# A PixArt block on one core: VectorE makes the low part of the contexts' query tokens, POOL adds the epsilon, and one small transfer goes ahead of another

## The chip, the core and the metric

The kernel runs on one core of a Trainium2 chip. The metric is the time of one execution on the device, in microseconds (us). The five engines have their own instruction queues and run side by side: TensorE (PE in the profile, with its weight loads as PEld), VectorE (DVE), ScalarE (ACT), GpSimd (POOL), and SyncE (SP), which here does nothing but issue transfers.

## What is computed

A transformer block over 16 samples of 256 tokens with 256 features, with a context of 256 tokens for each sample. Cut to what matters:

```
x_norm = modulate(_ln(x), shift_a, scale_a)
q, k, v = split(x_norm @ W_qkv + b_qkv)          # 16 heads of 16 features
x = x + gate_a * (softmax(q k^T * scale) v @ W_proj + b_proj)
q_c = _ln(x) @ W_qc + b_qc
k_c, v_c = split(_ln(context) @ W_kvc + b_kvc)
x = x + softmax(q_c k_c^T * scale) v_c @ W_cproj + b_cproj
h = gelu(modulate(_ln(x), shift_m, scale_m) @ W_mlp1 + b_mlp1)
x = x + gate_m * (h @ W_mlp2 + b_mlp2)
```

`_ln` is (x - mean) / sqrt(var + 1e-6). The change concerns `_ln(x)` ahead of `W_qc`: the tokens from which a context attention makes its queries.

## The kernel before

**Units and beats.** There are 32 attentions: for each sample one over its own tokens (kind "s") and one over its context (kind "c"). Each is a unit. They stand in the order s0 to s4, then s5, c0, s6, c1, ... s15, c10, and then c11 to c15 alone (lines 783 to 798). The main loop (lines 1241 to 1253) goes through the units, and through eight beats 0 to 7 in each; `beat(n, k)` (line 1073) writes out by hand what is issued in beat k of unit n. All engines keep the order in which the code is written. Behind the units stands the MLP, 16 samples in four chunks each.

**What a beat holds.** `visit` (line 1049) issues four matmuls of scores of the *next* unit into the PSUM tile `s` (`s_tile`, line 690) and four matmuls of transposed scores of the current unit into `st` (`t_part`). One VectorE reduction then takes the maxima of `s` (the tile `mx`), and one ScalarE instruction makes exponentials of `st` (the tile `pt`). There is one tile `s`, so the matmuls into it in a beat wait until the reduction of the beat before has read it; and `st` likewise waits for the exponentials. The even beats also hold 16 matmuls of probabilities by values (`av_part`, tile `o`) and the odd beats 24 matmuls of projections for units that are to come or that are done (`lanes`).

**Preparing a unit.** The unit n+3 is called q3, n+4 is q4; `lx` is q3 if it is a context unit, `lc` is q4 if it is one, `ls` is q4 if it is an "s" unit. For a context unit two layernorms are made: one of the context (`lc.ln[0]`, names with `_c`) and one of the tokens after the first attention (`lc.ln[1]`, names with `_q`). A layernorm (line 309) has three steps: `stats` (VectorE's bn_stats, tile `st_q`), `rstd` (VectorE's bn_aggr, tile `mv_q`, and then `pow`, tile `rs_q`: add epsilon, raise to -0.5) and `apply` (POOL, two instructions, tile `xn_q`). Adding epsilon is POOL's for samples 0 to 7 and VectorE's for samples 8 to 15 (the list `eased`, line 307); raising to the power is POOL's always.

**High and low part.** The normalized tokens are transposed by TensorE into PSUM (tile `psT_q`, in beat 4) and split in two numbers of lower precision: the high part `xTh_q` (ScalarE, `high`, line 385) and what is left, the low part `xTl_q`. For the context's query tokens ScalarE copies PSUM to the SBUF tile `y_q` (`full`, line 405), since POOL doesn't read PSUM here, and POOL subtracts (`rest_pool`, line 413). The function `low` (line 395) does the subtraction on VectorE, straight from PSUM; in `parts` (line 422) it is the third entry, and before the change it is used for the "s" units alone. Both parts are used in beat 1 of the next unit (tile `ps_qc`).

**Two rows on SP's queue.** In beat 0 the negated maxima of the second half (`m_row`, tile `m_1`) are sent into a row of the queries' tile, where beat 4 first uses them, and the softmax sums of the unit before are gathered (`pull_sums`, tile `S`). Their reciprocal is VectorE's in beat 2 (or 3, if q4 is an "s" unit); VectorE waits there if they have not landed.

**Where two context units follow each other.** For n = 23 to 28 the unit n+3 is a context unit, and for n = 23 to 27 so is the unit n+4. These six units then hold the work of `lx`, and all but the last also that of `lc`; before n = 23, units with the one and with the other alternate. `late` (line 1085) is set where `lc` is the first or the last sample.

Of the kernel before, what the change touches and what calls it, by code (L numbers as in the profile page):

```python
# [21 lines left out]
def pixart_block(  # L22
# [281 lines left out]
    class Box:  # L304
        pass

    eased = [f"{c}{b}" for c in "cq" for b in range(8, B)]

    def layernorm(src, name):

        o = Box()

        def stats():
            o.st = work.tile([P, NT, 6], F32, tag="bnst", bufs=4, name=f"st_{name}")
            for t in range(NT):
                DVE.bn_stats(o.st[:, t], src()[:, t])

        def rstd(power=True):
            o.mv = work.tile([P, NT, 2], F32, tag="bnmv", bufs=4, name=f"mv_{name}")
            for t in range(NT):  # L320
                DVE.bn_aggr(o.mv[:, t], o.st[:, t])
            o.rs = work.tile([P, NT], F32, tag="rstd", bufs=4, name=f"rs_{name}")
            if power:
                o.pow()

        def pow():
            if name in eased:
                DVE.scalar_tensor_tensor(o.rs, o.mv[:, :, 1], EPS, o.mv[:, :, 1], ALU.add, ALU.max)
            else:
                POOL.tensor_scalar(o.rs, o.mv[:, :, 1], EPS, None, ALU.add)  # L330
            POOL.tensor_tensor(o.rs, o.rs, mhalf, ALU.pow)

        def apply(eng=E_['LN'].get(name[0])):
            o.xn = work.tile([P, NT, H], F32, tag="xn", name=f"xn_{name}", bufs=3)
            if eng == "act":
                nb = work.tile([P, NT], F32, tag="rstd", name=f"nb_{name}", bufs=4)
                DVE.scalar_tensor_tensor(nb, o.mv[:, :, 0], -1.0, o.rs, ALU.mult, ALU.mult)
            for t in range(NT):
                if eng == "act":
                    ACT.activation(o.xn[:, t], src()[:, t], AF.Identity, bias=nb[:, t:t + 1],  # L340
                                   scale=o.rs[:, t:t + 1])
                else:
                    (DVE if eng == "dve" else POOL).tensor_scalar(
                        o.xn[:, t], src()[:, t], o.mv[:, t, 0:1], o.rs[:, t:t + 1],
                        ALU.subtract, ALU.mult)

        def apply_half(t):
            if t == 0:
                o.xn = work.tile([P, NT, H], F32, tag="xn", name=f"xn_{name}", bufs=3)
                POOL.tensor_scalar(o.xn[:, t], src()[:, t], o.mv[:, t, 0:1], o.rs[:, t:t + 1],  # L350
                                   ALU.subtract, ALU.mult)
            else:
                ACT.activation(o.xn[:, t], src()[:, t], AF.Identity, bias=o.nb[:, t:t + 1],
                               scale=o.rs[:, t:t + 1])

        def apply_bias():
            o.nb = work.tile([P, NT], F32, tag="rstd", name=f"nb_{name}", bufs=4)
            DVE.scalar_tensor_tensor(o.nb, o.mv[:, :, 0], -1.0, o.rs, ALU.mult, ALU.mult)

        o.apply_half, o.apply_bias = apply_half, apply_bias  # L360

        def stat(t):
            if t == 0:
                o.st = work.tile([P, NT, 6], F32, tag="bnst", bufs=4, name=f"st_{name}")
            DVE.bn_stats(o.st[:, t], src()[:, t])

        o.steps, o.pow, o.stat = [stats, rstd, apply], pow, stat
        return o

# [351 lines left out]
    def m_turn(u, hf, pst=None):  # L721

        if pst is None:
            pst = ps_gen(f"psm_{u.n}_{hf}", SHORT)
        PE.transpose(pst[:16, :P], u.mx[:, hf].rearrange("p r a t -> p (r a t)"), ident)
        return pst
# [25 lines left out]
    def exps():  # L752

        for f in later:
            f()
        later.clear()
# [316 lines left out]
    def beat(n, k):  # L1073
# [29 lines left out]
        if k == 0:  # L1103
            exps()
            if prev:
                av_part(prev, 3)
            if q3 and q3.ready:
                q3.T[0].place()
                pst = m_turn(cur, 1, q3.T[0].ps[:, N:])
                q3.T[0].turn((0,))  # L1110
            else:
                pst = m_turn(cur, 1)
            m_row(cur, 1, pst)
            if q2:
                q2.K.low()
            if prev:
                p1.pull_sums(1)
            if q2:
                q2.K.send_low()
            if p2:  # L1120
                p2.norm()
                p2.high()
                p2.low()
        elif k == 1:
            exps()
            run(lanes(q2 and q2.Q, q2 and n and q2.V))
            if prev:
                p1.pull_values(1)
            if lc:
                lc.ln[0].steps[0]()  # L1130
            if lx:
                if lx.b in (0, B - 1):
                    lx.ln[1].steps[0]()
                lx.ln[1].steps[1]()
                if lx.b == B - 1:
                    lx.ln[1].apply_half(0)
                else:
                    lx.ln[1].steps[2]()
        elif k == 2:
            exps()  # L1140
            if cur:
                av_part(cur, 0)
            if q3:
                q3.T[0].turn((1,) if q3.ready else (0, 1))
            if ls:
                ls.ln[0].steps[0]()
            elif prev:
                p1.recip()
                p1.spread()
            if not (q3 and q3.kind == "c"):  # L1150
                spare(n)
        elif k == 3:
            if q3:
                q3.T[0].high()
            exps()
            if q3 and q3.kind == "c":
                q3.T[0].full()
            if alone and p2:
                p2.proj(0)
                p2.proj(1)  # L1160
            elif n:
                run(lanes(p2, q2 and q2.Q))
            else:
                run(lanes(q2.V, q2.Q))
            if q3 and q3.kind == "s":
                q3.T[0].low()
            if prev and ls:
                p1.recip()
                p1.spread()
            if lx and lx.b == B - 1:  # L1170
                lx.ln[1].apply_bias()
        elif k == 4:
            if lx and lx.b == B - 1:
                lx.ln[1].apply_half(1)
            exps()
            if alone:
                p2.end()
            if cur:
                av_part(cur, 1)
            if lx:  # L1180
                lx.T[1].turn()
            if nxt:
                m_part(nxt, 0, st[:, 0] if lx else None)
            if q2:
                q2.Q.low()
                q2.Q.send_low()
            if q3 and q3.kind == "c":
                q3.T[0].rest_pool()
                spare(n, not lc)
            if ls:  # L1190
                ls.ln[0].steps[1]()
                ls.ln[0].steps[2]()
                ls.ready = True
        elif k == 5:
            exps()
            run(kp or lanes(q3 and q3.K, (None if alone else p2) if n else q2.V))
            if cur:
                o_out(cur, 0)
            if lc:
                lc.ln[0].steps[1]()  # L1200
                lc.ln[0].steps[2]()
                lc.ready = True
            v = unit(n + 5)
            if v and v.kind == "c":
                load(v)
            if prev:
                p1.back()
        elif k == 6:
            exps()
            if lx:  # L1210
                lx.T[1].high()
            if cur:
                cur.post.begin()
                av_part(cur, 2)
                cur.post.pull(0)
            if q3 and p2:
                q3.vk = lanes(q3.V, q3.K)
                run(q3.vk, 1)
            if p3:
                p3.store()  # L1220
            if lx:
                lx.T[1].full()
                lx.T[1].rest_pool()
                if lc:
                    p1.gate()
        elif k == 7:
            exps()
            run(q3.vk if q3 and p2 else lanes(q3 and q3.V, q3 and q3.K))
            if late:
                p2.add()  # L1230
                p2.added = True
            elif lc:
                lc.ln[1].steps[0]()
            v = unit(n + 5)
            if v and v.kind == "s":
                load(v)
            if n == nu - 1:
                p2.add()
                p2.store()
# [102 lines left out]
```

## Time and profile before

| | us |
|---|---|
| runs shown (three) | 730.75, 727.42, 733.64; median 730.75 |
| profiled execution, its own time | 729.14 |
| its span, first to last instruction | 727.3 |
| busy: PE, PEld, DVE, ACT, POOL | 712.7, 593.4, 566.5, 556.9, 538.9 |

The own time is 1.84 us more than the span, which lies around it. Rows of the timeline read: start in us, duration in us, engine, line, operation, tile written <- tiles read, shape, count, and in brackets the idle time of the engine before it with what ended it. Nearly all instructions carry line 51, that of the helper that records them, so the tiles' names tell them apart. Windows of time give the busy us of each engine in a stretch, with the number of its instructions.

### The profile page before, as it was taken

What the parts mean: (1) busy time and instruction counts of PE and PEld (TensorE: products, weight loads), DVE (VectorE), ACT (ScalarE), POOL (GpSimd) and SP (SyncE); (2) the same over time, 40 slices, a digit from 0 to 9 for tenths busy, and PEclk for the clock granted to TensorE, in tenths of its full rate; (3) what the DMA queues carried; (4) which work ended last, traced back from release to release, by engine and by line L of the source; (5) the groups of instructions that cost most, each with busy time, mean ns of one, the idle gap of its engine ahead of it and who ended that gap; (6) DMA issues with size and microseconds to landing.
All of it is one profiled execution on the core that took longest, in us unless ns stands there. A gap on an engine that the chain in (4) does not pass through costs nothing.

```text
span 727.3 us, 22494 instructions
## 1 busy us (share of the span) xinstructions
PE 712.7 (98%) x9007; PEld 593.4 (82%) x9007; DVE 566.5 (78%) x892; ACT 556.9 (77%) x971; POOL 538.9 (74%) x517
## 2 busy tenths in 40 slices
PE   9999999999999999999999999999999999999996
PEld 8777777877877778777777777777679999999996
DVE  4878888888887888888889888878675777777743
ACT  5677888888888888888888878888767677666661
POOL 8555788887866868787786797988767988666561
PEclk9999999999999999999999999999999999999999
DMA  7465455544545455454555645455332223213122
GB/s 253 151 223 172 151 173 169 186 170 164 166 149 185 155 188 194 157 164 164 192 170 181 205 152 178 149 183 184 97 88 94 89 59 88 72 61 89 52 51 73
DMA packets 81531, 106.14 MB, mean 146 GB/s; under 512 B 16594, under 2 KB 44532, under 8 KB 81428
## 3 DMA queue, kind: packets, MB, share of 16 engines
q1 hardware_dynamic: 80420, 104.12, 43.9%
q8 instruction: 71, 1.16, 0.7%
q10 hardware_dynamic: 1008, 0.59, 0.3%
q14 instruction: 32, 0.26, 0.1%
HBM read 35.89 MB, written 8.98 MB: 62 GB/s over the span
## 4 chain that ended last, share of the span: by engine, by line
PE 89%; DVE 5%; ACT 2%; DMA 1%; issue 1%; SPq 0%; ACTq 0%
PE s L51 18%; PE o L51 15%; PE st L51 14%; PE ph L51 12%; DVE mx L51 4%; PE ps_v_c L51 3%; PE ps_k L51 3%; PE ps_q L51 3%; PE ps_kc L51 3%; PE ps_P_s L51 3%; PE ps_v_s L51 3%; PE ps_qc L51 2%; PE ps_P_c L51 2%; PE psT_s L51 2%; PE psT_c L51 1%
## 5 line engine op out<-in xcount | busy, mean ns | idle before, releaser
L51 DVE TENSOR_REDUCE mx<-s 128x4 f32<-128x1024 f32 x252 | 308.0, 1222 | 81.2 <-PE s L51 79.5
L51 ACT ACTIVATE pt<-st 128x1024 f32<-128x1024 f32 x256 | 264.6, 1033 | 54.3 <-PE st L51 52.9
L51 PE MATMUL o<-pt,v 128*32 128x256 f32 x2048 | 137.0, 385 | 0.0
L51 PE MATMUL s<-big 63*128 63x256 f32 x1008 | 117.2, 306 | 6.2 <-DVE mx L51 5.0
L51 PE MATMUL st<-big 64*128 64x256 f32 (+1 forms) x1040 | 109.6, 285 | 0.7 <-ACT pt L51 0.7
L51 PE MATMUL ph<-xTh_m,wself 128*128 128x256 f32 x512 | 99.5, 280 | 0.0
L51 PEld LDWEIGHTS s<-big 63*128 63x128 f32 x1008 | 77.4, 185 | 25.5 <-DVE mx L51 11.2
L51 POOL TENSOR_TENSOR hl<-hf,hh 128x512 fp32r<-128x512 f32 x60 | 81.4, 1375 | 19.4 <-ACT hh L51 19.4
L51 PEld LDWEIGHTS o<-pt,v 128*32 128x32 f32 x2048 | 53.4, 109 | 39.4 <-ACT oT L51 0.8
L51 PEld LDWEIGHTS st<-big 64*128 64x128 f32 (+1 forms) x1040 | 81.2, 186 | 4.4 <-ACT pt L51 2.1
L51 PEld LDWEIGHTS ph<-xTh_m,wself 128*128 128x128 f32 x512 | 81.9, 188 | 1.2 <-issue 0.4
L51 PE MATMUL ph<-xTl_m,wself 128*128 128x256 f32 x256 | 70.9, 277 | 0.0
L51 ACT ACTIVATE hh<-ph,bT 128x256 fp32r<-128x256 f32 x112 | 47.4, 479 | 19.0 <-PE st L51 7.4
L51 ACT ACTIVATE hf<-ph,bT 128x256 f32<-128x256 f32 x112 | 47.2, 475 | 19.1 <-PE ph L51 19.0
L51 PEld LDWEIGHTS ph<-xTl_m,wself 128*128 128x128 f32 x256 | 48.2, 188 | 0.0
L51 PE MATMUL s<-big,hh 128*128 128x256 f32 x256 | 45.2, 277 | 0.0
L51 DVE TENSOR_SCALAR xn_m<-x,mv_m,rs_m 128x256 f32<-128x256 f32 x28 | 33.5, 1237 | 14.8 <-POOL rs_m L51 14.8
L51 POOL TENSOR_SCALAR xn_c<-c,mv_c,rs_c 128x256 f32<-128x256 f32 x32 | 39.0, 1228 | 1.7
L51 PE MATMUL st<-big,hh 128*128 128x256 f32 x224 | 39.5, 276 | 0.0
L51 POOL TENSOR_SCALAR xn_q<-x,mv_q,rs_q 128x256 f32<-128x256 f32 x31 | 37.8, 1228 | 1.7
L51 PEld LDWEIGHTS s<-big,hh 128*128 128x128 f32 x256 | 38.7, 188 | 0.0
L51 ACT COPY oT<-o 128x512 f32<-128x512 f32 x64 | 37.5, 587 | 1.4 <-PE o L51 1.4
(231 smaller groups left out, 2127.0 us busy)
## 6 DMA issues: line engine op xcount, KB each, us to landing
big<-h_kc SPq DMA_DIRECT2D x32, 256.0 KB
big<-h_qc SPq DMA_DIRECT2D x32, 256.0 KB
big<-h_k SPq DMA_DIRECT2D x31, 256.0 KB
big<-h_q SPq DMA_DIRECT2D x30, 256.0 KB
big<-l_k SPq DMA_DIRECT2D x16, 256.0 KB
g<-gd SPq DMA_DIRECT2D x16, 256.0 KB
U_s<-oT SPq DMA_DIRECT2D x32, 128.0 KB
c<-in_ctx_dram SPq DMA_DIRECT2D x16, 256.0 KB
```

The source lines that it names most:

```text
L51: i = f(*a, **k)
```

## The change

Four things are edited. Sixteen copies `y_q` by ScalarE and sixteen subtractions by POOL go away, and VectorE's `low` makes `xTl_q` from PSUM, in beat 7 instead of beat 6. The sixteen epsilon additions of `eased` go from VectorE to POOL. In beat 0 the gathering of the sums is issued on SP's queue ahead of the maxima's row. And where a unit has both `lx` and `lc`, the statistics `st_q` of `lc` are taken in beat 6 instead of beat 7.

```
-    eased = [f"{c}{b}" for c in "cq" for b in range(8, B)]
...
         def pow():
-            if name in eased:
-                DVE.scalar_tensor_tensor(o.rs, o.mv[:, :, 1], EPS, o.mv[:, :, 1], ALU.add, ALU.max)
-            else:
-                POOL.tensor_scalar(o.rs, o.mv[:, :, 1], EPS, None, ALU.add)
+            POOL.tensor_scalar(o.rs, o.mv[:, :, 1], EPS, None, ALU.add)
             POOL.tensor_tensor(o.rs, o.rs, mhalf, ALU.pow)
...
                 pst = m_turn(cur, 1)
+            if prev:
+                p1.pull_sums(1)
             m_row(cur, 1, pst)
             if q2:
                 q2.K.low()
-            if prev:
-                p1.pull_sums(1)
-            if q2:
                 q2.K.send_low()
...
             if lx:
-                lx.T[1].full()
-                lx.T[1].rest_pool()
                 if lc:
                     p1.gate()
+                    if not late:
+                        lc.ln[1].steps[0]()
         elif k == 7:
             exps()
+            if lx:
+                lx.T[1].parts[2]()
...
-            elif lc:
+            elif lc and not lx:
                 lc.ln[1].steps[0]()
```

TensorE's instructions and their order are the same in both. On VectorE, in unit 23's last two beats and unit 24's first three, this stood before (the numbers behind names are those of buffers; an epsilon addition is shown as TENSOR_SCALAR with the tile `rs_q`):

```order
L51 BN_STATS st_q_7965<-x_11_6822 128x6 x2
L51 TENSOR_REDUCE mx_7976<-s 128x2x2
L51 TENSOR_SCALAR l_kc_8001<-ps_kc_7843,bP,h_kc_7968 128x256 x2
L51 TENSOR_REDUCE mx_7976<-s 128x2x2
L51 BN_STATS st_c_8048<-c_7890 128x6 x2
L51 BN_AGGR mv_q_8051<-st_q_7965 128x2 x2
L51 TENSOR_SCALAR rs_q_8054<-mv_q_8051 128x2
L51 TENSOR_REDUCE mx_7976<-s 128x2x2
```

and this stands there now, one reduction further back at the start:

```order
L51 BN_STATS st_q_7909<-x_11_6804 128x6 x2
L51 TENSOR_REDUCE mx_7630<-s 128x2x2
L51 TENSOR_TENSOR xTl_q_7888<-psT_q_7808,xTh_q_7887 128x512
L51 TENSOR_REDUCE mx_7954<-s 128x2x2
L51 TENSOR_SCALAR l_kc_7980<-ps_kc_7823,bP,h_kc_7946 128x256 x2
L51 TENSOR_REDUCE mx_7954<-s 128x2x2
L51 BN_STATS st_c_8026<-c_7870 128x6 x2
L51 BN_AGGR mv_q_8029<-st_q_7909 128x2 x2
L51 TENSOR_REDUCE mx_7954<-s 128x2x2
```

The statistics have moved ahead of unit 23's last reduction, `xTl_q` stands where they stood, and nothing stands any more between `mv_q` and the third reduction of unit 24.

On POOL, from the end of unit 23 to the middle of unit 24, this stood before (`U_c`, `xTh_ac` and `xTl_ac` are the normalized output of the context attention two units back and its two parts):

```order
L51 TENSOR_TENSOR xTl_q_7908<-y_q_7929,xTh_q_7907 128x512
L51 TENSOR_TENSOR U_c_7599<-U_c_7599,R_c_7892 128x512
L51 COPY xTh_ac_8007<-U_c_7599 128x512
L51 TENSOR_TENSOR xTl_ac_8008<-U_c_7599,xTh_ac_8007 128x512
L51 TENSOR_TENSOR rs_q_8054<-rs_q_8054,mhalf 128x2
L51 TENSOR_SCALAR xn_q_8057<-x_11_6822,mv_q_8051,rs_q_8054 128x256 x2
```

and now:

```order
L51 COPY xTh_ac_7985<-U_c_7579 128x512
L51 TENSOR_TENSOR xTl_ac_7986<-U_c_7579,xTh_ac_7985 128x512
L51 TENSOR_SCALAR rs_q_8032<-mv_q_8029 128x2
L51 TENSOR_TENSOR rs_q_8032<-rs_q_8032,mhalf 128x2
L51 TENSOR_SCALAR xn_q_8035<-x_11_6804,mv_q_8029,rs_q_8032 128x256 x2
```

The subtraction has left the start of this piece, and the epsilon addition stands in front of the power.

On SP's queue, in beat 0 of unit 16, the piece was

```order
L51 DMA big_75<-h_kc_5462 32x4x512 x2
L51 DMA big_76<-m_1_5492 2x8x128
L51 DMA S_s_5419<-oT_5385 64x1x32
L51 DMA big_75<-l_kc_5495 32x4x512
L51 DMA U_s_5418<-oT_5385 64x512
```

and is

```order
L51 DMA big_75<-h_kc_5448 32x4x512 x2
L51 DMA S_s_5407<-oT_5373 64x1x32
L51 DMA big_76<-m_1_5479 2x8x128
L51 DMA big_75<-l_kc_5482 32x4x512
L51 DMA U_s_5406<-oT_5373 64x512
```

so that the sums `S` and the row `m_1` have changed places; this is so in every unit.

## The prediction, as put on record before the run

> **What bounds the kernel now.** I read the busy times first, then windows of time to see where TensorE isn't full, then its waits in those windows, then the timeline of the engine that it waits for. The first row is the page's, the two others are windows: start and end, length, and the busy us of PE, PEld, DVE, ACT and POOL.
>
> ```profile
> PE 712.7 (98%) x9007; PEld 593.4 (82%) x9007; DVE 566.5 (78%) x892; ACT 556.9 (77%) x971; POOL 538.9 (74%) x517
> ...
> 283.60:314.90 31.30, 31.30 (x468) 24.46 (x472) 26.23 (x41) 26.49 (x43) 24.55 (x25) 1.00 0.54 173
> ...
> 409.10:426.20 17.10, 16.06 (x239) 12.50 (x242) 14.55 (x24) 13.84 (x23) 14.62 (x14) 1.00 0.56 186
> ```
>
> TensorE is the bound at full clock (the 1.00). Where "s" and context units alternate, two units take 31.30 us and TensorE is busy in all of it: what the other engines save there is worth nothing unless a matmul starts earlier by it. The third window, one unit long (from beat 6 of unit 23 to beat 6 of unit 24), takes 17.10 us with 16.06 busy. The reader is to see that the change frees POOL and ScalarE, which are 74% and 77% busy and not the bound, and that what can be won is above all the missing microsecond of such units. The Trainium skill (Perfetto Trace Analysis, Identifying the Most-Contended Engine) would have TensorE judged by its weight loads rather than its matmuls, here 82% and not 98%; no run here tells which is the better measure, and the sum doesn't use it.
>
> These are TensorE's weight loads for the scores that waited for a maximum, in beat 3 of units 23 to 28; the bracket holds the wait.
>
> ```profile
> 402.24 0.30 PEld L51 LDWEIGHTS s<-big 63*128 63x128 f32 x4 [0.43 <-DVE mx L51]
> 419.29 0.30 PEld L51 LDWEIGHTS s<-big 63*128 63x128 f32 x4 [1.27 <-DVE mx L51]
> 435.99 0.30 PEld L51 LDWEIGHTS s<-big 63*128 63x128 f32 x4 [0.98 <-DVE mx L51]
> 452.94 0.30 PEld L51 LDWEIGHTS s<-big 63*128 63x128 f32 x4 [1.18 <-DVE mx L51]
> 469.67 0.30 PEld L51 LDWEIGHTS s<-big 63*128 63x128 f32 x4 [0.97 <-DVE mx L51]
> 485.77 0.30 PEld L51 LDWEIGHTS s<-big 63*128 63x128 f32 x4 [0.32 <-DVE mx L51]
> ```
>
> Why the maximum was late stands in VectorE's timeline of unit 24, and POOL's beside it; the five rows after that are the epsilon additions of the other five units.
>
> ```profile
> 416.60 0.23 DVE L51 BATCH_NORM_AGGREGATE mv_q<-st_q 128x2 f32<-128x6 f32 x2
> 416.86 1.24 DVE L51 SCALAR_TENSOR_TENSOR rs_q<-mv_q 128x2 f32<-128x2 f32 x1
> 418.02 1.21 DVE L51 TENSOR_REDUCE mx<-s 128x4 f32<-128x1024 f32 x1
> ...
> 416.80 1.28 POOL L51 TENSOR_TENSOR xTl_ac<-U_c,xTh_ac 128x512 fp32r<-128x512 f32 x1
> ...
> 400.62 0.44 DVE L51 SCALAR_TENSOR_TENSOR rs_q<-mv_q 128x2 f32<-128x2 f32 x1
> 433.92 0.89 DVE L51 SCALAR_TENSOR_TENSOR rs_q<-mv_q 128x2 f32<-128x2 f32 x1
> 450.63 1.12 DVE L51 SCALAR_TENSOR_TENSOR rs_q<-mv_q 128x2 f32<-128x2 f32 x1
> 467.56 0.93 DVE L51 SCALAR_TENSOR_TENSOR rs_q<-mv_q 128x2 f32<-128x2 f32 x1
> 484.43 0.16 DVE L51 SCALAR_TENSOR_TENSOR rs_q<-mv_q 128x2 f32<-128x2 f32 x1
> ```
>
> An addition of two numbers per partition takes 0.16 us in the last row and 1.24 in unit 24, where it starts 0.06 after a POOL subtraction and ends 0.02 after it (416.86 + 1.24 = 418.10; 416.80 + 1.28 = 418.08). It waits for POOL to be done. The maximum behind it is late by that much, and TensorE with it.
>
> **Epsilon on POOL.** With the addition gone, the maximum follows `mv_q`. In each unit TensorE gains the addition's time, but no more than it waited: 0.43 of 0.44, 1.24 of 1.27, 0.89, 1.12, 0.93 and 0.16; together 4.77. The other ten moved additions are those of the contexts and of samples 8 and 9. I cost them at nothing: they stand in beat 5, where the next maximum waits for TensorE and not for VectorE, or in the alternating units, whose window is full.
>
> What it costs is on POOL, where the price of one is in the first row here. Behind it wait the power, `xn_q`, and in beat 4 TensorE's transposes of `xn_q`.
>
> ```profile
> L51 POOL TENSOR_SCALAR rs_q<-mv_q x8: 229/229/230, 87.8 to 306.3; 128x2 f32<-128x2 f32 x8
> ...
> 418.99 2.44 POOL L51 TENSOR_SCALAR xn_q<-x,mv_q,rs_q 128x256 f32<-128x256 f32 x2
> ...
> 422.82 0.66 PE L51 MATMUL psT_q<-ident,xn_q 128*128 128x128 f32 x4
> ```
>
> In unit 24 `xn_q` ends at 418.99 + 2.44 = 421.43, and 0.23 and a gap of about 0.08 later with the addition: 421.74. TensorE came at 422.82 and now comes 1.24 earlier, at 421.58: a new wait of 0.16. In unit 26 the like is shorter, since the gain is 1.12 there; the others gain less and so leave more room. I take off 0.2 for all. VectorE's part is then **4.6 us**. The Trainium skill (Perfetto Trace Analysis, Optimizing GPSIMD Operations) speaks against this step: work should be on other engines where it can be, since GpSimd is generally slower. By the rows that holds only while POOL is still, 0.16 on VectorE against 0.23. By the rule the six additions would win nothing and cost 0.07 each, some 0.4 us in all; by the rows above they took 4.78 on VectorE, so I go with the rows.
>
> **The low part from PSUM on VectorE.** No row of before is this instruction. One bound is the same kind of operation with one operand in PSUM, at half the size; the other is the same subtraction with both in SBUF:
>
> ```profile
> L51 DVE TENSOR_TENSOR mt<-s,gm x16: 406/410/425, 561.4 to 716.7; 128x256 f32<-128x256 f32 x16
> ...
> L51 DVE TENSOR_TENSOR xTl_m<-xTf_m,xTh_m x15: 693/1144/1647, 534.4 to 698.1; 128x512 fp32r<-128x512 f32 x15
> ```
>
> From the first, 256 more elements: the maximum `mx` takes 1.21 for 1024, so 256 are at most 0.30, and 0.41 + 0.27 to 0.30 is 0.68 to 0.71. From the second, 0.69 to 1.65. I take 0.7, since the operands are those of the first, whose 16 never went over 0.425. The Trainium skill (SBUF — State Buffer, Who interferes with whom) draws the same line: with two SBUF inputs VectorE contends with GpSimd's reads, with at most one it doesn't. The traces agree as far as these two rows go, and in the 1.24 above, whose two inputs are both in SBUF.
>
> Where does it go? Here is beat 7 of unit 15 and beat 0 of unit 16 on VectorE and ScalarE, and the TensorE instructions that come next to need either.
>
> ```profile
> 285.21 1.23 DVE L51 TENSOR_REDUCE mx<-s 128x4 f32<-128x1024 f32 x1 [0.60 <-PE s L51]
> 287.03 1.23 DVE L51 TENSOR_REDUCE mx<-s 128x4 f32<-128x1024 f32 x1 [0.60 <-PE s L51]
> ...
> 285.21 0.64 ACT L51 COPY y_q<-psT_q 128x512 f32<-128x512 f32 x1
> 285.69 1.09 ACT L51 ACTIVATE pt<-st 128x1024 f32<-128x1024 f32 x1
> ...
> 288.27 0.28 PE L51 MATMUL psT_s<-ident,mx 128*16 128x128 f32 x1
> ...
> 288.70 0.51 PE L51 MATMUL s<-big 63*128 63x256 f32 x4
> ```
>
> VectorE is free from 286.44 (the rows overlap by some 0.08, so 286.36) to 287.03: 0.7 ends at 287.06. The next maximum then starts at most 0.05 late and ends by 288.31, and its matmuls come at 288.70. It costs nothing; up to 0.69 + 0.4 = 1.1 it would cost nothing. Its PSUM buffer is given back at 287.06 and is next written at 288.27. In units 23 to 26 the statistics stood in this gap; they go into the gap a beat earlier:
>
> ```profile
> 410.76 1.23 DVE L51 TENSOR_REDUCE mx<-s 128x4 f32<-128x1024 f32 x1 [0.60 <-PE s L51]
> 411.90 0.74 DVE L51 BATCH_NORM_STATS2 st_q<-x 128x6 f32<-128x256 f32 x2
> ...
> 457.96 1.29 POOL L51 TENSOR_TENSOR x<-xg,t_s 128x512 f32<-128x512 f32 x1
> 462.59 0.74 DVE L51 BATCH_NORM_STATS2 st_q<-x 128x6 f32<-128x256 f32 x2
> ```
>
> The 0.74 fit there in the idle 0.60 and the overlaps. What they read must be ready a beat earlier: the latest is sample 14's, ready at 457.96 + 1.29 = 459.25, read at 462.59 and now some 1.8 earlier, at 460.8, which the gain above brings to about 459.7. That holds by 0.4. I cost the move at nothing.
>
> On ScalarE the copy goes, and the exponentials of beat 7, which waited behind it, start when their matmuls are done. TensorE's chain in beat 0 of unit 16 (start, us) stands against that of unit 17, which has no such copy before it:
>
> ```profile
> 286.74 0.25 PE s L51 x4
> 286.99 0.35 PE st L51 x4
> ...
> 302.13 0.28 PE s L51 x4
> 302.41 0.23 PE st L51 x4
> ```
>
> 0.60 against 0.51: the matmuls into `st` wait about 0.1 for exponentials that end at 285.69 + 1.09 = 286.78. Sixteen units have the copy: 16 x 0.09 = **1.4 us**. Between nothing (if the 0.1 is something else) and 16 x 0.12 = 1.9 I take the difference of the rows. POOL's sixteen subtractions (beat 7) win nothing, as TensorE uses the low part in beat 1 only.
>
> **The sums ahead of the row.** On SP's queue S moves past `m_1` alone, and `m_1` is issued the later by S's issue.
>
> ```profile
> 289.18 0.58 SPq L51 DMA_DIRECT2D big<-m  x1
> 289.81 0.60 SPq L51 DMA_DIRECT2D S_s<-oT  x1
> ...
> 231.88 0.30 PEld L51 LDWEIGHTS s<-big 63*128 63x128 f32 x4 [0.91 <-DVE mx L51]
> ```
>
> S comes 0.6 earlier and `m_1` 0.6 later, which has until beat 4, some 8 us. In this execution S was late for TensorE once, in unit 12: VectorE waited for S in front of the maximum, and TensorE for that, 0.91. Earlier issue may win between nothing (if it is held by what is ahead of it in the same queues) and 0.63 (the whole of the move). I put it at 0 and keep 0.6 for the range.
>
> **The sum.** 729.1 (own time of the profiled execution) - 4.6 - 1.4 = **723.1 us**. The median of the three runs stands 1.6 above that execution; if this is in the kernel rather than that run, 724.7.
>
> **Rivals.**
> - *POOL's chain takes the gain.* It starts with a transfer, and if in units 24 and 26 that lands as late as before, `xn_q` is late by all that TensorE comes earlier, and by the 0.31 of the addition. Against it: the rows of unit 24 leave 1.08 of room. If it took all of the 4.6, the time would be 729.1 - 1.4 = 727.7.
> - *Slower: `xTl_q` is held by POOL.* If it takes the 1.65 of the longest `xTl_m`, the maximum of beat 0 is late by about 0.95, and TensorE by 0.5 in 11 alternating units (5.5) and by 0.8 in the five that follow (4.0), where VectorE has no gap before beat 3. 729.1 - 6.0 + 9.5 = 732.6. It decides from about 1.1 us on, and eats the gain from about 1.5. For it is only that the subtractions in the MLP vary so; against it the operand in PSUM, and that POOL's own subtraction is gone from that place.
> - *More: the sums were late often.* The runs shown differ by 6.2 us, and S is the one transfer seen to hold VectorE in the middle of a unit. If earlier issue takes off a microsecond or two more than the profiled execution shows, 721.3.
>
> **How the numbers follow.** The forecast has 0.62, the POOL chain 0.17, slower 0.08, more 0.13. From 720.0 (the last case, less the 1.3 that its own size may be off) to 729.0 (above POOL's chain by as much) some 0.15 is left out. About 1% (7.3 us) is what a measurement of this kernel tells from no change: faster by that has all of the last case and a third of the forecast (its 723.1 lies 1.2 from the border 721.9, and runs scatter more than that), 0.34; slower by that is half of its case, 0.04; within it 0.62.
>
> **What would show it.** Right: `rs_q` gone from VectorE, the waits in beat 3 of units 23 to 28 down from 5.15 us to under 0.6, the window of unit 24 at 15.9 us; `xTl_q` on VectorE at 0.7 us in all sixteen; TensorE's chain in beat 0 at 0.51 in place of 0.60. Wrong: `xTl_q` that varies, transposes `psT_q` that wait for `xn_q`, statistics in beat 6 that wait for POOL, or alternating units that are still 31.3 us for two.

## The result, and the profile after

The kernel before took 727.82 us here (median of 22 runs, 725.47 to 734.50), the changed one 724.05 (22 runs, 722.81 to 730.38). The ratio is 0.9948, with a 95% interval of 0.9928 to 0.9969: 3.8 us less, between 2.3 and 5.2. That is faster, and within the 1% that one such measurement of this kernel can tell.

The profiled execution of the changed kernel took 729.5 us and is one of four in 22 that lie above 728. Its first reduction came at 26.3 us, some 5.4 us later than in the execution before, in code that the change doesn't touch; what that was stands under the last experiments. The rest of it can be compared with the execution before piece by piece. The page's busy times:

```profile
PE 714.3 (98%) x9007; PEld 596.8 (82%) x9007; DVE 570.2 (78%) x892; ACT 550.2 (76%) x955; POOL 522.4 (72%) x517
```

The same two stretches as before the change, from beat 6 to beat 6 (start and end, length, and the busy us of PE, PEld, DVE, ACT, POOL):

```profile
288.03:319.27 31.24, 31.24 (x468) 24.44 (x471) 26.81 (x42) 26.06 (x42) 22.81 (x24) 1.00 0.53 174
412.95:428.80 15.85, 15.85 (x240) 12.43 (x239) 13.68 (x23) 13.42 (x22) 13.51 (x14) 1.00 0.58 197
```

Unit 24 went from 17.10 us to 15.85, and TensorE is now busy in all of it. Two alternating units went from 31.30 to 31.24. VectorE in unit 24: the maximum follows the statistics at once.

```profile
420.34 0.23 DVE L51 BATCH_NORM_AGGREGATE mv_q<-st_q 128x2 f32<-128x6 f32 x2
420.49 1.19 DVE L51 TENSOR_REDUCE mx<-s 128x4 f32<-128x1024 f32 x1
```

The weight loads in beat 3 of units 24 and 28, and the transposes in beat 4 of unit 27:

```profile
421.93 0.30 PEld L51 LDWEIGHTS s<-big 63*128 63x128 f32 x4 [0.17 <-DVE S_s L51]
...
473.08 0.14 PEld L51 LDWEIGHTS psT_q<-ident,xn_q 128*128 128x128 f32 x1 [0.41 <-POOL xn_q L51]
474.02 0.31 PEld L51 LDWEIGHTS psT_q<-ident,xn_q 128*128 128x128 f32 x3 [0.81 <-POOL xn_q L51]
...
486.22 0.30 PEld L51 LDWEIGHTS s<-big 63*128 63x128 f32 x4 [0.17 <-DVE mx L51]
```

The waits of beat 3 are down to 0.17 in each of the six units. That 0.17 is no wait for VectorE, though the bracket names it. The same 0.17 stands behind the transposes `psT_c` in beat 1 of these units, before the change as after, where the profile finds no engine that was waited for. Here is beat 1 of unit 24 before:

```profile
414.25 0.30 PEld L51 LDWEIGHTS s<-big 63*128 63x128 f32 x4 [0.17 <-issue]
```

In beat 3 it was part of the longer waits. Unit 27 has a new wait, 0.81, for `xn_q`. (The 0.41 before `psT_q` is there in every unit, mostly put down to issue.)

Where the time went is best seen in the starts of the 256 reductions `mx`, which stand in the same order in both. From the traces, start in the changed kernel minus start before:

| beat 0 of unit | start before, us | after minus before, us | what happened since the row above |
|---|---|---|---|
| 4 | 98.14 | +5.93 | the late start, 5.43 by the first reduction; 0.50 more in the units up to here |
| 12 | 223.42 | +5.57 | four copies `y_q` gone: -0.36 |
| 14 | 239.91 | +4.44 | unit 12 has no wait of 0.91 us behind S, and one more copy is gone: -1.13 |
| 23 | 396.45 | +4.13 | five copies gone: -0.31 |
| 24 | 412.58 | +3.86 | -0.27 |
| 25 | 429.63 | +2.66 | -1.20 |
| 26 | 446.36 | +1.81 | -0.85 |
| 27 | 463.27 | +0.76 | -1.05 |
| 28 | 480.07 | +0.63 | -0.13 |
| 29 | 497.00 | +0.32 | -0.31 |

Behind unit 29 both run alike (+0.23 at 513).

This sets one execution against one. The one before was long in just this place: from unit 23 to unit 29 it took 497.00 - 396.45 = 100.55 us. Two others in which the additions are still VectorE's took 98.24 and 98.66 there (sums_alone and eps_one_input, below).

### The profile page after: what moved, and what is told of

Read it like the earlier page. It is cut to its first block, busy times and chain, and to the rows that moved or that the text cites. A ratio compares the mean times of both kernels' runs of the same rounds, so it can differ in the third digit from the quotient of the medians.

```text
span 727.7 us, 22546 instructions
## 1 busy us (share of the span) xinstructions
PE 714.3 (98%) x9007; PEld 596.8 (82%) x9007; DVE 570.2 (78%) x892; ACT 550.2 (76%) x955; POOL 522.4 (72%) x517
## 4 chain that ended last, share of the span: by engine, by line
PE 93%; DVE 3%; ACT 1%; POOL 1%; DMA 1%; issue 1%; ACTq 0%; SPq 0%; POOLq 0%
PE s L51 18%; PE o L51 16%; PE st L51 15%; PE ph L51 12%; PE ps_q L51 4%; PE ps_k L51 4%; PE ps_qc L51 3%; PE ps_v_c L51 3%; PE ps_P_s L51 3%; PE ps_kc L51 3%; PE ps_v_s L51 3%; PE ps_P_c L51 2%; PE psT_c L51 2%; PE psT_s L51 2%; DVE mx L51 2%; PE psT_q L51 1%
## 5 line engine op out<-in xcount | busy, mean ns | idle before, releaser
L51 PE MATMUL st<-big 64*128 64x256 f32 (+1 forms) x1040 | 107.7, 282 | 0.7 <-ACT pt L51 0.7
L51 PE MATMUL ph<-xTl_m,wself 128*128 128x256 f32 x256 | 70.9, 277 | 0.0
L51 POOL TENSOR_TENSOR U_c<-U_c,R_c 128x512 f32<-128x512 f32 x15 | 19.4, 1295 | 29.7 <-DMA R_c<-rd_c 17.8
L51 PE MATMUL st<-big,hh 128*128 128x256 f32 x224 | 39.5, 276 | 0.0
```

The source lines that it names most:

```text
L51: i = f(*a, **k)
```

## Experiments

Four theories stood against each other at first: that the gain comes from the epsilon additions, from the low part, from the order of the two transfers, or from more than one. Then the reasons for each were tested, and last the late start. All ratios are against the kernel before on the same chip.

**One part at a time.** First the epsilon additions on POOL alone:

```
-    eased = [f"{c}{b}" for c in "cq" for b in range(8, B)]
...
-            if name in eased: DVE.scalar_tensor_tensor(o.rs, ...)
+            POOL.tensor_scalar(o.rs, o.mv[:, :, 1], EPS, None, ALU.add)
```

> The kernel before with one part of the change: all epsilon additions on POOL. If the additions that waited on VectorE for POOL are the gain, the waits of TensorE in beat 3 of units 23 to 28 go from 5.15 us to under 0.6 and the time falls by 2.5 to 4.5 us; less than the 4.6 of the prediction, since POOL still has the low part to make and xn_q comes later, so that transposes may wait for it. If the gain is the work taken off ScalarE and POOL, the time stays within 1 us of before.

Measured: 727.09 us (12 runs, 724.46 to 728.54), ratio 0.9971 (0.9950 to 0.9991). The advice that the prediction quoted against this step (the Trainium skill, Perfetto Trace Analysis, Optimizing GPSIMD Operations) isn't borne out here: by it the step would have cost some 0.4 us, and it won about 2. That is less than the 2.5 to 4.5 expected, though the interval (0.7 to 3.6 us) overlaps this. In its trace the waits of beat 3 are down to 0.17 each, and the transposes of unit 25 wait 1.02 for `xn_q`.

Then the low part from PSUM on VectorE, with the statistics in beat 6, alone:

```
-                lx.T[1].full()
-                lx.T[1].rest_pool()
+                    if not late: lc.ln[1].steps[0]()      # in beat 6
...
+                lx.T[1].parts[2]()                        # in beat 7
```

> The kernel before with the low part on VectorE from PSUM and the statistics in beat 6, the additions and the sums as before. If the additions are the gain, this brings 0.7 to 1.4 us (the matmuls into st in beat 0 of sixteen units, 0.05 to 0.09 each) and rs_q still takes up to 1.2 us on VectorE. If the work taken off POOL is the gain, POOL's subtractions move ahead of rs_q, rs_q takes 0.16, and most of the 4 us come with this part.

Measured: 727.12 us (12 runs, 724.75 to 730.57), ratio 0.9976 (0.9958 to 0.9995). Here the additions are still VectorE's:

```profile
L51 DVE SCALAR_TENSOR_TENSOR rs_q<-mv_q x8: 160/506/1058, 336.5 to 480.9; 128x2 f32<-128x2 f32 x8
```

In units 23 to 28 they took 0.16, 0.16, 0.39, 0.62, 0.86 and 1.06, instead of 0.44, 1.24, 0.89, 1.12, 0.93 and 0.16. With POOL's sixteen subtractions gone, other additions are the long ones: taking work off POOL doesn't cure them.

Last the sums ahead of the row, alone:

```
+            if prev: p1.pull_sums(1)
             m_row(cur, 1, pst)
-            if prev: p1.pull_sums(1)
```

> The kernel before with the sums issued ahead of the row, nothing else. By the prediction it is worth 0 to 0.6 us in an execution in which a sum is late, so no difference that can be told (ratio 0.999 to 1.001). By the rival that the sums are often late, 1 to 2 us less.

Measured: 728.39 us (12 runs, 726.06 to 730.38), ratio 0.9994 (0.9976 to 1.0012): no difference that can be told. TensorE's 0.91 us wait behind S was seen in the profiled execution before alone; three others with S in its old place (eps_alone, low_alone, eps_one_input) have none in that unit.

This run shows something else too. The additions are untouched in it, and unit 24's took 0.16, not 1.24:

```profile
416.45 0.16 DVE L51 SCALAR_TENSOR_TENSOR rs_q<-mv_q 128x2 f32<-128x2 f32 x1
```

The six of units 23 to 28 took 0.28, 0.16, 0.16, 0.55, 0.90 and 0.17, together 2.22 us where the execution before had 4.78. In low_alone they took 3.25, and in eps_one_input, the next run, 2.93. What the additions cost varies from execution to execution, and the prediction had read the longest of these four.

So the additions and the low part bring about 0.3% and 0.2%, and together the 0.5% of the change.

**Does the small addition wait because it has two inputs in SBUF?** The prediction had it so. Before the change, with one tensor input instead of two:

```
-                DVE.scalar_tensor_tensor(o.rs, o.mv[:, :, 1], EPS, o.mv[:, :, 1], ALU.add, ALU.max)
+                DVE.tensor_scalar(o.rs, o.mv[:, :, 1], EPS, None, ALU.add)
```

> The kernel before with the additions still on VectorE, but as an operation with one tensor input and a constant in place of the same tensor twice (add, then maximum of that and the tensor itself). If VectorE waits for POOL because both its inputs come from SBUF, all sixteen take 0.1 to 0.2 us, whatever POOL does, and most of the 4 us come without moving anything to POOL. If any operation of VectorE on these two numbers waits for POOL, they still take up to 1.2 us and the time is that of before.

Measured: 728.32 us (12 runs, 726.13 to 728.93), ratio 0.9996 (0.9979 to 1.0013). Unit 25 on VectorE, with POOL beside it:

```profile
432.93 0.90 DVE L51 TENSOR_SCALAR rs_q<-mv_q 128x2 f32<-128x2 f32 x1
```

```profile
432.51 1.28 POOL L51 TENSOR_TENSOR xTl_as<-U_s,xTh_as 128x512 fp32r<-128x512 f32 x1
```

It starts 0.42 after POOL's subtraction and ends 0.04 after it (433.83 against 433.79); where POOL is just ending, it takes 0.17. The reason with the two inputs fell; that it waits for POOL stands. The Trainium skill (SBUF — State Buffer, Who interferes with whom) would have said so, had the prediction taken up the other half of its rule: a `tensor_scalar` may go into a mode that uses VectorE's second pair of ports, and then it contends with GpSimd too. The 0.90 agrees.

**Is it the PSUM operand that keeps `xTl_q` at 0.68?** In the changed kernel:

```profile
L51 DVE TENSOR_TENSOR xTl_q<-psT_q,xTh_q x16: 678/680/681, 103.4 to 496.4; 128x512 fp32r<-128x512 f32 x16
```

The experiment brings ScalarE's copy back, and VectorE subtracts from it, both operands in SBUF:

```
+                lx.T[1].full()               # ScalarE copies psT_q to y_q again
...
-                lx.T[1].parts[2]()
+                lx.T[1].rest_pool(DVE)       # VectorE: xTl_q = y_q - xTh_q
```

> The changed kernel, but ScalarE makes the copy y_q again and VectorE subtracts from that, so that both inputs of the subtraction are in SBUF; place and size are the same. If the operand in PSUM is what keeps the subtraction at 0.68 us, it now varies between 0.69 and 1.9 with what POOL does in beat 7, and the time rises by 1 to 4 us over the changed kernel. If the place where POOL was cleared is what keeps it so, it stays near 0.69 and only the copy costs, about 1 us.

Measured: 726.21 us (10 runs, 723.84 to 730.31), ratio 0.9971 (0.9951 to 0.9991), some 1.7 us above the changed kernel. VectorE's sixteen, and POOL beside the one at 462.75:

```profile
L51 DVE TENSOR_TENSOR xTl_q<-y_q,xTh_q x16: 680/681/684, 102.0 to 495.2; 128x512 fp32r<-128x512 f32 x16
```

```profile
461.68 2.85 POOL L51 TENSOR_SCALAR xn_c<-c,mv_c,rs_c 128x256 f32<-128x256 f32 x2
```

With both operands in SBUF it is 0.68 as well. Where POOL was busy in this beat it ran `xn_c` or `xn_s`, which take one tensor and scalars, and such a one didn't hold VectorE, with up to 0.58 us beside it; POOL's own next instruction was late here, 2.85 for two in place of 2.44. So the place keeps it at 0.68, and in this place the PSUM operand isn't needed for that. Next to a POOL *subtraction* it probably would be: the MLP of the changed kernel has both kinds beside each other, POOL first, then VectorE.

```profile
571.46 1.29 POOL L51 TENSOR_TENSOR xTl_ac<-U_c,xTh_ac 128x512 fp32r<-128x512 f32 x1
572.71 1.75 POOL L51 TENSOR_TENSOR hl<-hf,hh 128x512 fp32r<-128x512 f32 x1
```

```profile
572.02 1.28 DVE L51 TENSOR_TENSOR xTl_m<-xTf_m,xTh_m 128x512 fp32r<-128x512 f32 x1 [1.15 <-ACT xTh_m L51]
573.22 0.74 DVE L51 TENSOR_TENSOR mt<-st,gm 128x256 f32<-128x256 f32 x2
```

`xTl_m`, both operands in SBUF, takes 1.28 beside POOL's first subtraction and 0.69 alone. The two `mt`, one operand in PSUM, take 0.74 beside the second, and 0.74 where POOL is still.

**What are the statistics worth in beat 6?** The changed kernel with `st_q` left in beat 7, behind `xTl_q`:

```
-                    if not late: lc.ln[1].steps[0]()      # in beat 6
...
-            elif lc and not lx:
+            elif lc:
```

> The changed kernel with the statistics st_q left in beat 7 for units 23 to 26, behind the subtraction there. By the gap read from the profile (0.60 us) both together don't fit: the maximum of beat 0 is late by some 0.65, TensorE waits 0.2 to 0.5 in each of four units, 1 to 2 us in all over the changed kernel. If VectorE has room enough in these units without the additions, no difference.

Measured: 726.62 us (10 runs, 725.53 to 727.33), ratio 0.9979 (0.9964 to 0.9993), some 2.2 us above the changed kernel. Unit 24, beat 1:

```profile
412.22 0.30 PEld L51 LDWEIGHTS s<-big 63*128 63x128 f32 x4 [0.46 <-DVE mx L51]
413.00 0.18 PEld L51 LDWEIGHTS ps_qc<-xTh_q,wqch 64*128 64x128 f32 x1 [0.25 <-DVE l_kc L51]
```

The gap holds one of the two, not both: 0.46 + 0.25 here, and 0.44 and about 0.25 in each of the units 25 to 27, 2.8 us in the trace. Of each of the first ones 0.17 stands there in any case, so some 2.1 us are lost.

**Why did unit 27 win only 0.13?** POOL's chain there, in the changed kernel, and what SP had issued for it:

```profile
466.96 1.30 POOL L51 TENSOR_TENSOR U_s<-U_s,R_s 128x512 f32<-128x512 f32 x1 [1.79 <-DMA R_s<-rd_s]
...
471.53 2.44 POOL L51 TENSOR_SCALAR xn_q<-x,mv_q,rs_q 128x256 f32<-128x256 f32 x2
```

```profile
459.67 1.53 SPq L51 DMA_DIRECT2D c<-in_ctx_dram  x1
461.31 0.68 SPq L51 DMA_DIRECT2D R_s<-rd_s  x1
```

POOL waited 1.79 us for the reciprocal sums R, whose issue stood behind the load of a context that took SP 1.53. The chain then ran through, and `xn_q` ended at 473.97, the moment from which TensorE's transposes went on (474.02). The experiment puts R's transfer first:

```
+            if prev: p1.back()           # R, ahead of the load of the next context
             ...
-            if prev: p1.back()
```

> The changed kernel, with the transfer R (reciprocals spread over the partitions) issued ahead of the next context's load in beat 5, where it stood behind it. In unit 27 of the changed kernel TensorE lost about 0.8 us in beat 4, waiting for xn_q, which stood behind U_s, which waited 1.79 for R. If R is what is late there, POOL's waits for R shrink by about 0.7 us each, unit 27 no longer waits, and the time falls by 0.6 to 0.9 us. If the landing is set by what the queues hold and not by the issue, no difference.

Measured: 724.97 us (8 runs, 722.11 to 725.67), ratio 0.9948 (0.9930 to 0.9967). The wait is gone from the trace and units 24 to 28 gained 4.3 us in place of 3.5, but 0.8 us is less than these runs resolve. Nor does every execution with R in its old place have this wait: of the five other profiled ones (stats_late, low_from_sbuf, start_held, start_held2, hold_unused) four lose nothing at these transposes, and start_held2 loses 0.6 in two units.

**The late start.** VectorE's first normalization, before and after, and POOL in the changed kernel:

```profile
6.54 0.74 DVE L51 TENSOR_SCALAR xn_s<-x,mv_s,rs_s 128x256 f32<-128x256 f32 x2 [1.16 <-POOL rs_s L51]
```

```profile
6.52 3.54 DVE L51 TENSOR_SCALAR xn_s<-x,mv_s,rs_s 128x256 f32<-128x256 f32 x2 [1.15 <-POOL rs_s L51]
```

```profile
6.88 1.29 POOL L51 TENSOR_TENSOR wself<-wf,wself 128x512 fp32r<-128x512 f32 x1 [0.40 <-ACT wself L51]
8.11 1.81 POOL L51 MEMSET big<- 128x2048 f32 x1
```

`xn_s` ended at 10.06, just behind POOL's two instructions (9.92). In the execution before they began at 7.81, after `xn_s`. The first of them reads what ScalarE makes of the weights (`wself`). ScalarE did that earlier here: its work before it waited for TensorE until 5.93, and until 6.79 in the execution before.

VectorE's 2.8 us (10.06 for 7.28) are only about half of the 5.4. With `xn_s` late, TensorE was busy for 2.45 of the 5 us from 5 to 10 (4.91 before). Soon after, its granted clock fell to half, the 0.50 behind the engines' times here (the changed kernel, then before). It was 0.65 on average in the 5 us before these and 0.82 in the 5 us after, so half speed lasted some 10 us.

```profile
15.00:20.00 5.00, 5.00 (x25) 5.00 (x25) 2.33 (x11) 1.92 (x4) 4.12 (x6) 0.50 0.18 66
...
15.00:20.00 5.00, 4.43 (x38) 4.04 (x37) 3.36 (x11) 3.16 (x7) 3.38 (x4) 1.00 0.64 231
```

The mean clock of a whole run tells the late starts. The three profiled executions that started late have 0.991 to 0.995, all others 0.998 or more. Of the changed kernel's runs the four above 728 have 0.991 to 0.994, and the other eighteen 0.998 or more. The kernel before has such runs as well, 7 of the 97 beside the experiments (0.992 to 0.995), so they aren't the change's alone. To hold POOL's two instructions back, the changed kernel with a POOL copy of 8 bytes per partition that has to wait for `xn_s`:

```
+    hold = const.tile([P, 2], F32, name="hold")
...
+        if i == 1:
+            POOL.tensor_copy(hold, u0.ln[0].xn[:, 1, :2])
```

> The changed kernel, with a POOL copy of two numbers of the first normalized tokens ahead of the low part of the keys' weights, so that POOL cannot begin that before VectorE has made those tokens. In the profiled execution of the changed kernel this first normalization took 3.54 us on VectorE in place of 0.74, beside a POOL subtraction and a memset that began 0.36 us into it, and the first maximum came 5.44 us later than in the profiled execution of before. If that is the cause of the executions near 729 us, they are gone and all lie between 722 and 726; the fast ones are no slower by more than 0.3. If the start is late for another reason, such executions stay, about one in four.

Measured: 730.58 us (12 runs, 729.48 to 731.41), ratio 1.0025 (1.0008 to 1.0042). The start was early and the twelve runs agree within 2 us, but some 6 us were lost in the MLP. The experiment had two edits in one: the copy, and a tile that moves every tile placed after it. So the tile alone, which nothing uses:

```
+    hold = const.tile([P, 2], F32, name="hold")
```

> The changed kernel with the new tile of 8 bytes per partition only, and no instruction that uses it. If the place of the later tiles costs start_held its 6 us, the ratio is 1.002 (about 730) and the matmuls ph in the MLP take 284 ns on average; if the copy costs them, this is the changed kernel again, 0.995.

Measured: 731.07 us (7 runs, 729.28 to 737.00), ratio 1.0053 (1.0027 to 1.0079). Two groups of the MLP's matmuls (busy us, mean ns), in the changed kernel and then with the unused tile:

```profile
L51 PE MATMUL ph<-xTh_m,wself 128*128 128x256 f32 x512 | 99.5, 280 | 0.0
...
L51 PE MATMUL s<-big,hh 128*128 128x256 f32 x256 | 45.2, 277 | 0.0
```

```profile
L51 PE MATMUL ph<-xTh_m,wself 128*128 128x256 f32 x512 | 102.6, 284 | 0.0
...
L51 PE MATMUL s<-big,hh 128*128 128x256 f32 x256 | 46.7, 281 | 0.0
```

Each matmul is 4 ns longer. These two groups are busy 3.1 and 1.5 us more; the MLP's other two large ones (`ph` from `xTl_m`, 70.9 to 71.9, and `st` from `hh`, 39.5 to 40.9) add 1.0 and 1.4, in all the 7.0 us by which the medians differ. So the place of the tiles costs it, and start_held's time told nothing of the copy. The copy then went into a tile that was there already:

```
+        if i == 1:
+            POOL.tensor_copy(dummy, u0.ln[0].xn[:, 1, :2])
```

> The changed kernel with the same POOL copy ahead of the second subtraction of the weights' low parts as in start_held, written into a tile that is there already, so that no tile is placed elsewhere. If the copy takes away the late starts and the 6 us of start_held came from the new tile's place, VectorE's first normalization takes 0.4 us each in the profile, TensorE's matmuls ph in the MLP go back to a mean of 280 ns, the time is a ratio of 0.994 to 0.995 and its highest run stays under 726 us instead of 730. If the copy itself costs the 6 us, the ratio is again 1.002 and ph at 284 ns.

Measured: 723.39 us (6 runs, 722.90 to 725.75), ratio 0.9946 (0.9929 to 0.9964). With R's transfer first as well (the edit of back_first):

> The changed kernel with R's transfer ahead of the context's (back_first) and the copy of start_held2. If both gains add, unit 27 has no wait of the transposes psT_q for xn_q, no run stands above 726, and the median is 722.5 to 723.5, a ratio of 0.993 to 0.994. If the unit's 0.8 us was luck of that profile, the same as start_held2.

Measured: 722.68 us (6 runs, 722.17 to 723.95), ratio 0.9933 (0.9916 to 0.9949), the best of all. `xn_s` took 0.74 in its profile, and unit 27 has no wait for `xn_q`. It stands 0.7 us under start_held2, which is what back_first won in the trace; the intervals overlap, so the times alone don't settle it.

The last one forces the meeting, with an instruction of POOL's that only writes. It is back_first, and in the order at the start the clearing of `big` comes first:

```
-L0b b1 L0d scale hik lok T0t z1kp b2
+L0b z1kp b1 L0d scale hik lok T0t b2
```

> The kernel of back_first (R's transfer ahead of the context's) with POOL's clearing of the tile big, 1.8 us, ahead of the keys' low weights instead of behind them, so that it runs beside VectorE's first normalization xn_s in every run, and the subtraction comes only after it. If a POOL instruction that only writes holds VectorE as the subtraction does, xn_s x2 takes 2.2 to 2.6 us in place of 0.74 and ends near 8.4 to 8.9, so the start is late by 1.1 to 1.9 us, the same in every run: 723.8 to 724.8, a ratio of 0.994 to 0.996. If only the subtraction holds it, xn_s stays at 0.74, no run is late, and the time is that of both2: 722.2 to 723.2, 0.992 to 0.994.

Measured: 729.60 us (12 runs, 726.34 to 731.36), ratio 1.0009 (0.9984 to 1.0034). VectorE, and POOL beside it:

```profile
6.53 3.16 DVE L51 TENSOR_SCALAR xn_s<-x,mv_s,rs_s 128x256 f32<-128x256 f32 x2 [1.15 <-POOL rs_s L51]
```

```profile
6.44 1.80 POOL L51 MEMSET big<- 128x2048 f32 x1
8.22 1.32 POOL L51 TENSOR_TENSOR wself<-wf,wself 128x512 fp32r<-128x512 f32 x1
```

More than either theory expected. The first of the two normalizations took 1.87 us beside the clearing, and the second 1.38 beside the subtraction, which comes at once behind it. `xn_s` ends at 9.69, after both (9.54), 2.4 us later than in back_first, and the first maximum comes 4.1 us later. Again TensorE's clock goes with the rest: it was 0.57 from 10 to 15 us and 0.75 from 15 to 20, where back_first had 1.00. All twelve runs are over 726, and they lie by their mean clock: 726.3 to 727.8 where it is 0.994 or 0.995, 729.5 to 731.4 where it is 0.988 to 0.990. So what POOL does beside the first normalization makes the late start, and the halved clock goes with the rest of it. That the clock falls because TensorE had too little to do is likely, but no run tried it by itself. In the changed kernel, whether the two meet is left to when ScalarE is done. Of the four kernels that leave it to that with their tiles in place (the changed one, low_from_sbuf, stats_late, back_first), 6 of 50 runs have the low clock; of start_held, start_held2 and both2, none of 24. With the 7 of 97 of the kernel before, 24 without one may still be chance, so that the copy rids the kernel of them is likely, not proved.

## Why the prediction was right, and where it was not

The time came out at 724.05 for 723.1, inside the range, faster but within 1%. The mechanism was right, but the number is closer than its parts. The gain was 3.8 us (2.3 to 5.2), not 6.0, and the base, 729.1, stood 1.3 above the median of before, so two errors cancelled in part. They are not independent. Base and gain were read in the same execution, and what it lost more than others in units 23 to 28 stands in both.

- **The addition waits for POOL, and the maximum for it: right.** eps_alone shows it by itself, and the window of unit 24 is 15.85 for the 15.9 forecast.
- **"TensorE gains the addition's time, but no more than it waited", 4.77 us: the step that failed, by its size.** The additions took 4.78 us in the execution that was read, and 2.22, 2.93 and 3.25 in the three others that have them on VectorE. eps_alone's runs put the gain at 2.1 (0.7 to 3.6). And of each wait 0.17 was never the addition's, as it stands behind the transposes in any case: the six waits of 5.15 give 5.15 - 6 x 0.17 = 4.1 even in that execution. "Under 0.6" for what would be left of them was therefore wrong as well: 1.0.
- **"I take off 0.2 for all": too little in this execution.** The room behind `xn_q` was read in unit 24, where R lands in time. In unit 27 it didn't, and 0.8 us were lost there alone. The rival "POOL's chain takes the gain" named the right link, a transfer that lands late; it took one unit of six here, and nothing in four of the five other executions with R in its old place. In both2, without that wait, unit 27 won 0.92, its copy included.
- **The copies, 16 x 0.09: about right, 0.07.** Nine copies in the alternating units won 0.36 + 0.31 = 0.67 in the trace after. TensorE's chain in beat 0 of unit 16 is now

```profile
291.18 0.24 PE s L51 x4
291.42 0.23 PE st L51 x4
```

0.47 in place of 0.60, so 0.13 was won there, not 0.09. Some of it is given back in beat 1: from the reduction of beat 0 to that of beat 1 it is now 2.10 us for 2.22 before, and from there to beat 2 it is 1.94 for 1.86. VectorE between the first two:

```profile
292.61 0.87 DVE L51 SCALAR_TENSOR_TENSOR l_kc<-ps_kc,bP,h_kc 128x256 fp32r<-128x256 f32 x2
293.56 1.23 DVE L51 TENSOR_REDUCE mx<-s 128x4 f32<-128x1024 f32 x1
```

VectorE has no gap left there; before, it waited 0.21 for TensorE. That `l_kc` is what is late next was only read here, though stats_late shows TensorE waiting for it.
- **`xTl_q` at 0.7, hidden: right in size (0.678 to 0.681, sixteen times) and in cost; the reason was half right.** The PSUM operand does keep VectorE out of POOL's way, as `mt` shows, but in this place it had nothing to keep out of.
- **The statistics in beat 6, at nothing: right**, and needed, as stats_late shows.
- **The sums: right at 0** as far as the runs tell; the rival "late often" isn't borne out by sums_alone (0.4 us less, between 1.7 less and 0.9 more).
- **Slower by POOL's hold: didn't come.** Its condition was a POOL subtraction beside `xTl_q`; there is none in that beat.

Added up for the two traces: 3.8 in units 23 to 28, their six copies included, and 0.7 for the ten other copies make 4.5. The runs gave 3.8, and the execution before was long in those units.

## What to carry to other kernels

An instruction of a sixth of a microsecond can cost more than a whole one, if it stands behind another engine's long instruction and in front of what TensorE waits for: look for the one whose duration varies, set its end beside the other engine's ends, and move it to that engine. Take a duration that varies from several executions before you add it up. Of a wait that goes, count only what is above the idle time that stands in such a place in any case, and read the room behind the next link in every unit that shall gain, not in one. A late start can cost twice: here 2.8 us of VectorE's were followed by a halved clock of TensorE's. An experiment that adds a tile also moves the tiles behind it: write into one that is there, or run the bare tile beside it.

## What was not expected of the hardware

VectorE's normalization of 128x256, 0.41 us alone, was held by a POOL instruction that only writes (1.87 us in memset_first, beside the clearing), and one was held through two POOL instructions in a row (3.22 in the changed kernel).

A late start of VectorE by 2.8 us was followed by TensorE's clock at 0.50 for some 10 us, and the first maximum was 5.4 us late.

An unused tile of 8 bytes per partition made the MLP's matmuls 4 ns longer each and the kernel some 7 us slower than the changed one. Which operand's place does it was not tried.
